# Layer 1's transformed signs at a row pitch of 32 words, and the high weight parts in float16 on the words' upper halves

## The chip, the cores and the metric

The kernel runs on one core of a Trainium2 chip. The metric is the device time of one execution in microseconds (us); three runs of the kernel before took 992.37, 992.5 and 993.49, median 992.5.

## The reference

Four layers are applied one after another to x of 16 images with 256 channels of 28 x 28. Layer 0 is a 3x3 convolution of signs with signs of weights and a batch norm. Layer 1, which the change concerns, is this (bn with stored moments is a scale s and a shift c per channel):

```
residual = prelu(x, a_alpha1)
z = hardsign(x + a_move)                      # sign(x): -1, 0 or 1
bw = clip(a_w, -1.0, 1.0)
y = conv_general_dilated(z, bw, 3x3, padding 1)
y = prelu(bn(y, a_bn1), a_alpha2)
y = se_gate(...) * y * residual
y = bn(y, a_bn2) + residual
z2 = hardsign(y + f_move)
u = einsum('bchw,oc->bohw', z2, clip(f_w))    # a 1x1 convolution
u = bn(se_gate(...) * prelu(bn(u, f_bn1), f_alpha2), f_bn2)
return u + y
```

Layer 2 is two more 3x3 convolutions of signs with batch norms, layer 3 attention over the 784 pixels of each image. In layer 1 the signs are whole numbers, but the weights are not[...].

## The kernel before

All work is on one core, and in stages: layer 0 to about 120 us, layer 1 from 123.6 to about 490 us, the two convolutions of layer 2 to about 700 us, and attention. The order of the instructions on TensorE (PE), VectorE (DVE) and ScalarE (ACT) is written out by hand in each stage (`manual_schedule`); on the queue of SyncE (SP) loads are issued, on that of GpSimd (POOL) stores of finished images.

**The convolution of layer 1.** It is computed by a transform over pairs of rows. From the padded signs of an image (`pads`, bfloat16), `transform` (DVE; the operation itself stands in the helper `tt`, so the profile shows L134) makes four sets u = 0 to 3 of 14 rows, sums or differences of two rows, with values between -2 and 2, and puts them into `vs`. This tile holds, in float32r (32-bit words[...]), for two images in turn, four sets and two groups of 128 channels, 14 rows of 30 words (28 columns and one more at each side). Set u is convolved along the row only, with three taps c = 0, 1, 2; the row of tap c begins c words later. The transformed weights are split into a high part `w1[0]`, rounded to float32r, and a low part `w1[1]`, the rest, both in float32r; this is done in layer 0, four pieces at a time: the sums of taps on DVE, `high` on ACT (L512), `low` on DVE (L516), in the list of side steps that `sign_layer` interleaves with the blocks of layer 0. `conv` (L699) sums over two channel groups k, the two parts and three taps: 12 matmuls of 128x128 weights with 128x392 rows into one half of an accumulator:

```
for k in range(2):
    for w in w1:
        for c in range(3):
            T.matmul(ps..., lhsT=w[:, k, c, u, mo*P:(mo+1)*P],
                     rhs=vs[:, b % 2, u, k, :, c:c + S], ...)
```

So three high matmuls alternate with three low ones. An image has two halves mo of output channels with four sets u each: 8 convolutions, 96 matmuls; 16 images make 1536.

**An iteration of layer 1** (`iteration(b)`) carries three images at different steps. PE's order: convolutions u = 1, 2 for mo = 0 (the first pair), u = 0, two small products (L618, hidden layer of the gates), u = 3, two small products (L778, gates), u = 1, 2, 0, 3 for mo = 1, and the 1x1 convolution of the image before (`conv1x1`, L809, 16 matmuls, also in float32r, with 392 words in a row). A pair shares one accumulator tile of two banks ("cv"). There are three such tiles and an iteration uses six, so a pair waits until the tile of three uses earlier is read out. The first pair of the next iteration reuses that of u = 0, 3 with mo = 1.

ACT takes t = s1 * (first of pair) + c1 (`sum_pair_a`, L720); DVE then makes t + s1 * (second) and t - s1 * (second) (`sum_pair_b`, L730, into `uvs`), and when u = 0, 3 are done adds these in (`rows_out`, L739), which frees the tile. Between these DVE has, for the neighbouring images, `enter` (L663), `prelu` (L751), `residual_b` (L691, which needs rn of ACT's L657), four transforms, `branch1_b` (L794) and `branch2` (L831). In iterations 1 to 6 it also packs signs of layer 2's second weights (`signs3`, L267), whose ACT results go through a stage tile of the tag "sgb".

When the operation counts its own doubts to be too large, a second, careful pass of the whole forward function follows; its `careful` branches are not run here.

Of the kernel before, what the change touches and what calls it, by code (L numbers as in the profile page):

```python
# [27 lines left out]
F32 = mybir.dt.float32  # L28
FR = mybir.dt.float32r
F16 = mybir.dt.float16  # L30
BF16 = mybir.dt.bfloat16
I16 = mybir.dt.int16
I32 = mybir.dt.int32
AF = mybir.ActivationFunctionType
ALU = mybir.AluOpType
# [4 lines left out]
P = 128  # L40
B = 16
S = 28
N = S * S
HN = N // 2
HR = S // 2
# [38 lines left out]
def forward(ctx: ExitStack, tc: tile.TileContext, d: dict, out: bass.AP, careful: bool):  # L84
# [4 lines left out]
    V, A, T = nc.vector, nc.scalar, nc.tensor  # L89
# [11 lines left out]
    def pv(name):  # L101
        return vec[:, VECS.index(name), :]
# [27 lines left out]
    def vtile(name):  # L130
        return const.tile([P, 2], F32, name=name)

    def tt(o, a, b, op):
        V.tensor_tensor(o, a, b, op)  # L134
        return o
# [284 lines left out]
    with tc.tile_pool(name="ps_conv", bufs=3, space=PSUM) as psc, \  # L420
# [13 lines left out]
        with tc.tile_pool(name="ph1", bufs=1) as ph:  # L434
# [51 lines left out]

            w1 = [ph.tile([P, 2, 3, 4, 256], FR, name=f"w1_{i}") for i in range(2)]
            fw = [ph.tile([P, 2, 256], FR, name=f"fw_{i}") for i in range(2)]  # L490

            def w1_step(k, c):
                sts, parts = [], []

                def load():
                    sts.append(xpool.tile([P, 3, 256], F32, tag="x2", name="st", bufs=3))
                    nc.sync.dma_start(out=sts[0], in_=d["w1"][k, :, c::3, :])

                def sums_of_taps():
                    st = sts[0]  # L500
                    V.tensor_scalar(st, st, -1.0, 1.0, ALU.max, ALU.min)
                    t = ph.tile([P, 3, 256], F32, tag="rn", name="asm", bufs=2)
                    a, s, m = (t[:, i, :] for i in range(3))
                    tt(a, st[:, 0, :], st[:, 2, :], ALU.add)
                    tt(s, a, st[:, 1, :], ALU.add)
                    tt(m, a, st[:, 1, :], ALU.subtract)
                    for u, (w, f) in enumerate(((st[:, 0, :], 1.0), (s, 0.5), (m, 0.5), (st[:, 2, :], -1.0))):
                        parts.append((w, f, *(x[:, k, c, u, :] for x in w1)))

                def high():  # L510
                    for w, f, hi, lo in parts:
                        A.activation(hi, w, AF.Copy, scale=f)  # L512

                def low():
                    for w, f, hi, lo in parts:
                        V.scalar_tensor_tensor(lo, w, f, hi.bitcast(F32), ALU.mult, ALU.subtract)  # L516

                return Step(load, sums_of_taps), high, low

# [12 lines left out]
            s1, s2, s3, s4 = (s_bn[:, i, :] for i in range(4))  # L532
            c1, c2, c3, c4 = (c_bn[:, i, :] for i in range(4))
            cc, zb2 = vtile("cc"), vtile("zb2")
            ra1, ra2, rf2, ns1 = (vtile(q) for q in ("ra1", "ra2", "rf2", "ns1"))
            mix_x, mix_y, mix_c = (const.tile([P, 2, 2], F32, name=n) for n in ("mix_x", "mix_y", "mix_c"))

            w_1, w_2, b_1 = (ph.tile(sh, F32, name=n) for sh, n in (([P, 2, P], "se1"), ([P, 256], "se2"), ([64, 1], "seb")))
# [4 lines left out]
            def constants():  # L543
                for p in pads:
                    nc.gpsimd.memset(p, 0.0)
                nc.gpsimd.tensor_copy(
                    doubts[:, 4 * NB:4 * NB + 6], vec[:, VECS.index("a1"):VECS.index("a3") + 1, :].rearrange("p i k -> p (i k)")
                )
                for i, n in enumerate(("a_alpha2", "f_alpha2")):
                    nc.gpsimd.tensor_copy(doubts[:, 4 * NB + 6 + 2 * i:4 * NB + 8 + 2 * i], pv(n))  # L550
                v = const.tile([P, 4, 2], F32, name="v_bn")
                for i, bn in enumerate(bns):
                    V.tensor_scalar(v[:, 2 * i:2 * i + 2], bn[:, 3::4], EPS, None, ALU.add)
                r = rsqrt("bn", v)
                for i, bn in enumerate(bns):
                    two = slice(2 * i, 2 * i + 2)
                    tt(s_bn[:, two], bn[:, 0::4], r[:, two], ALU.mult)
                    tt(c_bn[:, two], bn[:, 2::4], s_bn[:, two], ALU.mult)
                    tt(c_bn[:, two], bn[:, 1::4], c_bn[:, two], ALU.subtract)
                tt(cc, c2, c4, ALU.add)  # L560

                for o, q in ((ra1, "a_alpha1"), (ra2, "a_alpha2"), (rf2, "f_alpha2")):
                    V.tensor_scalar(o, pv(q), -1.0, 1.0, ALU.mult, ALU.add)
                V.tensor_scalar(ns1, s1, -1.0, None, ALU.mult)
                tt(zb2, c2, pv("f_move"), ALU.add)
                for g, (q, scale) in enumerate((("a", pv("a_scale")), ("f", pv("f_scale")))):
                    V.tensor_scalar(mix_x[:, g], scale, 1.0 / N, None, ALU.mult)
                    V.tensor_scalar(mix_y[:, g], scale, -1.0 / N, 1.0 / N, ALU.mult, ALU.add)
                    rows = slice(32 * g, 32 * g + 32)
                    nc.sync.dma_start(out=w_1[:, :, rows], in_=d[f"se1_{q}"])  # L570
                    nc.sync.dma_start(out=w_2[rows], in_=d[f"se2_{q}"])
                    nc.sync.dma_start(out=b_1[rows], in_=d[f"seb_{q}"])
                    nc.sync.dma_start(out=w_2[64 + 32 * g:65 + 32 * g], in_=d[f"seb2_{q}"])
                tt(mix_c[:, 1], pv("f_scale"), c2, ALU.mult)
# [48 lines left out]
                    rows = slice(32 * g, 32 * g + 32)  # L623
                    tt(b_1[rows], h, b_1[rows], ALU.add)

            vs = ph.tile([P, 2, 4, 2, HR, S + 2], FR, tag="vs", name="vs")

            def room_sums():
                return ph.tile([P, PIECE], F32, tag="sts", name="sts", bufs=2)

            if not careful:
                w2b = packed_weights(wpool, tag="wb")
                signs3 = sign_weights(ph, w2b, d["w2b"], ("sts", 2), sg=("sgb", 1))
            sums12 = weight_sums(room_sums, d["w2a_rows"], sf1, 6) + weight_sums(room_sums, d["w2b_rows"], sf2, 12)

            sums = {}
# [36 lines left out]
            def transform(b, u, k=slice(0, 2)):  # L673

                rows = pads[b % 2].rearrange("p k (i two) c -> p k two i c", two=2)
                e, o = rows[:, :, 0], rows[:, :, 1]
                e0, e1, o0, o1 = e[:, :, 0:HR], e[:, :, 1:HR + 1], o[:, :, 0:HR], o[:, :, 1:HR + 1]
                x, y, op = (
                    (e0, e1, ALU.subtract), (o0, e1, ALU.add), (e1, o0, ALU.subtract), (o0, o1, ALU.subtract)
                )[u]  # L680
                tt(vs[:, b % 2, u, k], x[:, k], y[:, k], op)

            rx = {}

# [8 lines left out]
            def conv(b, mo, u, ps):  # L693

                n = 0
                for k in range(2):
                    for w in w1:
                        for c in range(3):
                            T.matmul(  # L699
                                ps.rearrange("p (a b) -> p a b", b=S),  # L700
                                lhsT=w[:, k, c, u, mo * P:(mo + 1) * P],
                                rhs=vs[:, b % 2, u, k, :, c:c + S],
                                start=(n == 0),
                                stop=(n == 11),
                            )
                            n += 1
# [4 lines left out]
            pairs = {}  # L711
# [6 lines left out]
            def sum_pair_a(b, mo):  # L718
                t = temp("t1")[:, :HN]
                A.activation(  # L720
                    t, pairs[b, mo, True][:, 0, :HN], AF.Identity, bias=c1[:, mo:mo + 1], scale=s1[:, mo:mo + 1]
                )
                pairs[b, mo] = t

            def sum_pair_b(b, mo):

                ps, t = pairs.pop((b, mo, True)), pairs.pop((b, mo))
                uv = uvs[:, mo]
                for i, s in enumerate((s1, ns1)):
                    V.scalar_tensor_tensor(uv[:, i], ps[:, 1, :HN], s[:, mo:mo + 1], t, ALU.mult, ALU.add)  # L730
                pairs[b, mo] = uv

            def rows_out(b, mo):
                ps, uv = pairs.pop((b, mo, False)), pairs.pop((b, mo))
                y = full("yu", f"y{b}_{mo}", 6)
                ys[b, mo] = y
                two = y.rearrange("p (a two b) -> p two a b", two=2, b=S)
                for i in range(2):
                    V.scalar_tensor_tensor(  # L739
                        two[:, i], ps[:, i, :HN].rearrange("p (a b) -> p a b", b=S), s1[:, mo:mo + 1],  # L740
                        uv[:, i].rearrange("p (a b) -> p a b", b=S), ALU.mult, ALU.add,
                    )

# [203 lines left out]
            with tc.manual_schedule(engines={ET.PE, ET.DVE, ET.Activation}):  # L947
# [21 lines left out]
                b = B - 1  # L969
# [74 lines left out]
        with tc.tile_pool(name="ph2", bufs=1) as ph:  # L1044
            if careful:
                w2b = packed_weights(ph, tag="wb")
# [687 lines left out]
```

## Time and profile before

| | us |
|---|---|
| runs | 992.37, 992.5, 993.49 (median 992.5) |
| profiled execution, its own time | 991.88 |
| its span in the trace | 989.8 |
| PE busy, all of the kernel | 959.3 |
| DVE busy | 799.7 |
| ACT busy | 676.6 |
| layer 1's convolution (L699), PE busy, 1536 matmuls | 301.4 |
| 1x1 convolution (L809), PE busy, 256 matmuls | 49.1 |
| iteration 0 of layer 1 (123.62 to 142.32) | 18.7 |
| iterations 1 to 14, each | 21.9 to 22.0 |

How to read it: the profiler records one execution. "Busy" of PE is the union of its matmuls; these overlap, so the mean duration of one is longer than the distance between the starts of two, and it is that distance which adds up in a stream. PEld are the loads of weights, which lie beside the matmuls. A group's line gives the source line, engine, operation, output <- inputs, shapes, count, then busy us and mean ns of one, and behind the second bar the idle time of the engine before these instructions with what ended it. A timeline line gives start, duration, engine, line and operation, and in brackets the idle time before and what released it. Lines L134 and L148 are helpers, named with the tiles they work on. The granted clock of TensorE is full in layer 1 (1.00 in each stretch).

### The profile page before, as it was taken

How to read it: one execution, taken by the hardware profiler on the slowest of the kernel's cores; microseconds unless marked ns; L12 is line 12 of the kernel's file. 1: busy time of each engine (PE TensorE's matmuls, PEld its weight loads, DVE VectorE, ACT ScalarE, POOL GpSimd, SP SyncE). 2: the span in 40 equal slices, each digit the busy share in tenths (PEclk: the TensorE clock that was granted, in tenths of full speed). 3: DMA queues.
4: the chain of work that ended last, by engine and by line, in shares of the span. 5: the costliest groups of instructions: out<-in, count | busy, mean ns of one | idle time of the engine just before them, and what ended most of it. 6: DMA issues, size and time to landing. Idle time of an engine off the chain costs nothing.

```text
span 989.8 us, 14752 instructions
## 1 busy us (share of the span) xinstructions
PE 959.3 (97%) x5609; PEld 662.7 (67%) x5615; DVE 799.7 (81%) x1416; ACT 676.6 (68%) x1135; POOL 140.9 (14%) x149
## 2 busy tenths in 40 slices
PE   7999899999999999999999999999999999999995
PEld 3555499999999999999555555555444444444442
DVE  4766998999999899996779997999847777777765
ACT  6787437677776666664688877888676666666652
POOL 3000100000000000000000000000054434444430
PEclk9999999999999999999999999999999999999998
DMA  9877512334343322101291000000034252525212
GB/s 348 323 256 282 180 46 85 114 114 140 132 142 114 106 98 82 66 33 53 101 404 62 1 1 1 1 2 1 1 66 98 66 131 66 131 66 130 66 66 102
DMA packets 26949, 105.82 MB, mean 107 GB/s; under 512 B 3491, under 2 KB 7269, under 8 KB 26869
## 3 DMA queue, kind: packets, MB, share of 16 engines
q1 hardware_dynamic: 20948, 73.44, 20.8%
q0 software_dynamic: 5632, 30.54, 11.3%
q8 instruction: 46, 0.75, 0.3%
q10 hardware_dynamic: 288, 0.80, 0.2%
q14 instruction: 35, 0.28, 0.1%
HBM read 72.67 MB, written 32.11 MB: 106 GB/s over the span
## 4 chain that ended last, share of the span: by engine, by line
PE 45%; DVE 4%; ACT 1%; issue 1%; DVEq 0%; ACTq 0%
PE cv L340 19%; PE sc L1309 8%; PE av L1330 8%; PE mi L1286 4%; PE sm L1372 2%; PE mi L1390 2%; PE sm L1330 1%; DVE p L1096 1%; DVE r L1356 1%; DVE ab L354 0%; DVE l2c_fin L1098 0%; DVE l2b_fin L1098 0%; DVE p L1273 0%; PE sc L1390 0%; DVE p L1272 0%
## 5 line engine op out<-in xcount | busy, mean ns | idle before, releaser
L340 PE MATMUL cv<-fpads,wpk 128*128 128x392 f16 (+1 forms) x1746 | 295.7, 331 | 10.1 <-ACT fpads L451 5.1
L699 PE MATMUL cv<-vs,w 128*128 128x392 f32 x1536 | 301.4, 354 | 3.0 <-DVE vs L134 3.0
L699 PEld LDWEIGHTS cv<-vs,w 128*128 128x128 f32 x1536 | 287.3, 190 | 4.8 <-issue 3.4
L340 PEld LDWEIGHTS <-wpk 128*128 128x128 f16 x1746 | 168.9, 97 | 137.3 <-issue 9.8
L1313 ACT ACTIVATE es<-sc 128x784 f32<-128x784 f32 x112 | 87.3, 822 | 41.7 <-PE sc L1309 41.7
L1309 PE MATMUL sc<-q,keyswa 64*128 64x392 f32 x448 | 89.9, 513 | 0.9 <-ACT es L1313 0.9
L1096 DVE SCALAR_TENSOR_TENSOR p<-ab,vec 128x392 f32<-128x392 f32 x128 | 79.1, 618 | 2.3
L1330 PE MATMUL av<-es,v 128*64 128x392 f32 x448 | 80.7, 499 | 0.0
L1309 PEld LDWEIGHTS sc<-q,keyswa 64*128 64x128 f32 x448 | 38.9, 186 | 43.9 <-issue 17.1
L1323 POOL TENSOR_TENSOR sum<-sum,es 128x784 f32<-128x784 f32 x32 | 67.2, 2100 | 3.1 <-ACT es L1313 0.7
L134 DVE TENSOR_TENSOR vs<-pad 128x840 fp32r<-128x840 bf16 (+1 forms) x66 | 64.4, 1000 | 0.1
L1330 PEld LDWEIGHTS av<-es,v 128*64 128x64 f32 x448 | 29.4, 136 | 47.3 <-issue 47.0
L837 POOL DMA_DIRECT2D x2d<-x x16 | 8.6, 536 | 358.3 <-DVE x L831 295.0
L1297 DVE COPY keyswa<-mi 64x392 f32<-64x392 f32 x31 | 16.3, 565 | 52.5 <-ACT q L1293 52.5
L720 ACT ACTIVATE t<-cv,c_bn,s_bn 128x392 f32<-128x392 f32 x32 | 21.7, 678 | 49.9 <-PE cv L699 49.9
L351 ACT ACTIVATE t<-cv,rounding 128x392 f32<-128x392 f32 (+2 forms) x82 | 51.6, 630 | 4.9 <-PE cv L340 1.9
L1101 ACT ACTIVATE t<-ab 128x392 f32<-128x392 f32 x64 | 33.5, 524 | 27.8 <-DVE ab L354 27.8
L809 PE MATMUL cv<-z,fw 128*128 128x392 f32 x256 | 49.1, 343 | 1.0 <-ACT z L801 0.9
L354 DVE SCALAR_TENSOR_TENSOR ab<-ab,cv 128x392 f32<-128x392 f32 x64 | 35.4, 554 | 17.6 <-ACT ab L352 17.6
L809 PEld LDWEIGHTS cv<-z,fw 128*128 128x128 f32 x256 | 46.0, 188 | 2.2 <-ACT z L801 2.2
L1286 PE MATMUL mi<-p,wqk 128*128 128x392 f32 x124 | 45.3, 506 | 0.3 <-DVE p L1273 0.3
L1321 POOL TENSOR_TENSOR sum<-es 128x784 f32<-128x784 f32 x16 | 30.0, 1877 | 91.0 <-ACT es L1313 91.0
(284 smaller groups left out, 1462.7 us busy)
## 6 DMA issues: line engine op xcount, KB each, us to landing
xs<-in_x_dram SPq DMA_DIRECT2D x30, 784.0 KB, 6.8
x2d<-x POOLq DMA_DIRECT2D x16, 784.0 KB, 3.8
out_dram<-p SPq DMA_DIRECT2D x15, 784.0 KB, 3.7
p<-x2d POOLq DMA_DIRECT2D x14, 784.0 KB, 6.8
p<-x2d SPq DMA_DIRECT2D x13, 784.0 KB, 15.9
n0d<-n POOLq DMA_DIRECT2D x16, 392.0 KB, 4.8
n<-n0d SPq DMA_DIRECT2D x16, 392.0 KB, 3.1
st<-in_w_dram SPq DMA_DIRECT2D x12, 384.0 KB, 6.2
```

What stands on the lines that cost most here:

```text
L134: V.tensor_tensor(o, a, b, op)
L340: T.matmul(pss[j][:, n // size if careful else h, :rows * S].rearrange("p (a b) -> p a b", b=S), lhsT=w[:, n, t, :], rhs=pads[:, blocks[j] ...
L351: A.activation(by_halves(t, blocks[j]), ps, AF.Identity, bias=rounding, scale=1.0 / PACK)
L354: V.scalar_tensor_tensor(a, b, -PACK, ps, ALU.mult, ALU.add)
L699: T.matmul(ps.rearrange("p (a b) -> p a b", b=S), lhsT=w[:, k, c, u, mo * P:(mo + 1) * P], rhs=vs[:, b % 2, u, k, :, c:c + S], start=(n == 0),
L809: T.matmul(ps[:, h, :HN], lhsT=w[:, k, mo * P:(mo + 1) * P], rhs=z2[b][:, k, h * HN:(h + 1) * HN], start=(k + i == 0), stop=(k + i == 2),)
L1096: V.scalar_tensor_tensor(p, y, alpha[:, mo:mo + 1], y, ALU.mult, ALU.max)
L1286: T.matmul(ps[:, h, :HN], lhsT=wqk[:, k, :], rhs=x[b][:, k, h * HN:(h + 1) * HN], start=(k == 0), stop=(k == 1))
L1309: T.matmul(ps[:, h, :HN], lhsT=chunk[rows], rhs=qs[b][rows], start=True, stop=True)
L1313: A.activation(e, ps[:, :, :HN], AF.Exp, scale=0.125)
L1323: (V if late else nc.gpsimd).tensor_tensor(sums[b, late], sums[b, late], e, ALU.add)
L1330: T.matmul(ps[64 * h:64 * h + 64, :HN], lhsT=w, rhs=e[:, h, :], start=start, stop=stop)
```

## The change

The rows of `vs` stand at a pitch of 32 words in place of 30 (`WIDE = S + 4`; columns 0 to 29 are written, 30 and 31 are never read). The high part `w1[0]` becomes float16; so that small values keep their digits, high and low part are both made 2^15 times as large (`UP`), and the scales that read the accumulators are divided by that (`us1`, one DVE operation more, and `ns1`). The high matmuls don't read the float32r words but `vs16`, a bfloat16 view of the same tile that takes the upper half of each word; values between -2 and 2 in steps of one are the same in it. The low matmuls read the words as before. In the compiled program the float16 weights have load instructions of their own in PE's list, while a float32r matmul brings its load with it; otherwise the order of the work on PE, ACT, DVE, POOL and SP is the same. The stage tile of `signs3` takes the tag "sg" that layer 0's `signs2` used before it.

```diff
+            HI = FR if careful else F16
+            UP = 1.0 if careful else 2.0**15
-            w1 = [ph.tile([P, 2, 3, 4, 256], FR, name=f"w1_{i}") for i in range(2)]
+            w1 = [ph.tile([P, 2, 3, 4, 256], dt, name=f"w1_{i}") for i, dt in enumerate((HI, FR))]
...
                 def high():
                     for w, f, hi, lo in parts:
-                        A.activation(hi, w, AF.Copy, scale=f)
+                        A.activation(hi, w, AF.Copy, scale=f * UP)
 
                 def low():
                     for w, f, hi, lo in parts:
-                        V.scalar_tensor_tensor(lo, w, f, hi.bitcast(F32), ALU.mult, ALU.subtract)
+                        V.scalar_tensor_tensor(
+                            lo, w, f * UP, hi.bitcast(F32) if careful else hi, ALU.mult, ALU.subtract
+                        )
...
-                V.tensor_scalar(ns1, s1, -1.0, None, ALU.mult)
+                V.tensor_scalar(us1, s1, 1.0 / UP, None, ALU.mult)
+                V.tensor_scalar(ns1, s1, -1.0 / UP, None, ALU.mult)
...
-            vs = ph.tile([P, 2, 4, 2, HR, S + 2], FR, tag="vs", name="vs")
+            WIDE = S + 4
+            vs = ph.tile([P, 2, 4, 2, HR, WIDE], FR, tag="vs", name="vs")
+            vs16 = vs.rearrange("p b u k i c -> p (b u k i c)").bitcast(BF16).rearrange(
+                "p (b u k i c two) -> p b u k i c two", b=2, u=4, k=2, i=HR, two=2
+            )[..., 1]
...
-                signs3 = sign_weights(ph, w2b, d["w2b"], ("sts", 2), sg=("sgb", 1))
+                signs3 = sign_weights(ph, w2b, d["w2b"], ("sts", 2), sg=("sg", 1))
...
-                tt(vs[:, b % 2, u, k], x[:, k], y[:, k], op)
+                tt(vs[:, b % 2, u, k, :, 0:S + 2], x[:, k], y[:, k], op)
...
-                    for w in w1:
+                    for w, v in zip(w1, (vs if careful else vs16, vs)):
                         for c in range(3):
                             T.matmul(
                                 ps.rearrange("p (a b) -> p a b", b=S),
                                 lhsT=w[:, k, c, u, mo * P:(mo + 1) * P],
-                                rhs=vs[:, b % 2, u, k, :, c:c + S],
+                                rhs=v[:, b % 2, u, k, :, c:c + S],
```

In `sum_pair_a`, `sum_pair_b` and `rows_out`, `us1` takes the place of `s1`.

More of the change, by code (lines that the diff above doesn't have):

```diff
@@ L534, in forward @@
             cc, zb2 = vtile("cc"), vtile("zb2")
-            ra1, ra2, rf2, ns1 = (vtile(q) for q in ("ra1", "ra2", "rf2", "ns1"))
+            ra1, ra2, rf2, us1, ns1 = (vtile(q) for q in ("ra1", "ra2", "rf2", "us1", "ns1"))
             mix_x, mix_y, mix_c = (const.tile([P, 2, 2], F32, name=n) for n in ("mix_x", "mix_y", "mix_c"))
@@ L720, in sum_pair_a @@
                 A.activation(
-                    t, pairs[b, mo, True][:, 0, :HN], AF.Identity, bias=c1[:, mo:mo + 1], scale=s1[:, mo:mo + 1]
+                    t, pairs[b, mo, True][:, 0, :HN], AF.Identity, bias=c1[:, mo:mo + 1], scale=us1[:, mo:mo + 1]
                 )
@@ L728, in sum_pair_b @@
                 uv = uvs[:, mo]
-                for i, s in enumerate((s1, ns1)):
+                for i, s in enumerate((us1, ns1)):
                     V.scalar_tensor_tensor(uv[:, i], ps[:, 1, :HN], s[:, mo:mo + 1], t, ALU.mult, ALU.add)
@@ L739, in rows_out @@
                     V.scalar_tensor_tensor(
-                        two[:, i], ps[:, i, :HN].rearrange("p (a b) -> p a b", b=S), s1[:, mo:mo + 1],
+                        two[:, i], ps[:, i, :HN].rearrange("p (a b) -> p a b", b=S), us1[:, mo:mo + 1],
                         uv[:, i].rearrange("p (a b) -> p a b", b=S), ALU.mult, ALU.add,
```

## The prediction

> **What bounds the kernel now.** I read the page first, for the shares of the engines and the costliest groups:
>
> ```profile
> PE 959.3 (97%) x5609; PEld 662.7 (67%) x5615; DVE 799.7 (81%) x1416; ACT 676.6 (68%) x1135; POOL 140.9 (14%) x149
> ...
> L340 PE MATMUL cv<-fpads,wpk 128*128 128x392 f16 (+1 forms) x1746 | 295.7, 331 | 10.1 <-ACT fpads L451 5.1
> L699 PE MATMUL cv<-vs,w 128*128 128x392 f32 x1536 | 301.4, 354 | 3.0 <-DVE vs L134 3.0
> L699 PEld LDWEIGHTS cv<-vs,w 128*128 128x128 f32 x1536 | 287.3, 190 | 4.8 <-issue 3.4
> L340 PEld LDWEIGHTS <-wpk 128*128 128x128 f16 x1746 | 168.9, 97 | 137.3 <-issue 9.8
> ...
> L809 PE MATMUL cv<-z,fw 128*128 128x392 f32 x256 | 49.1, 343 | 1.0 <-ACT z L801 0.9
> ```
>
> The convolution of layer 1 (L699) keeps TensorE busy for 301.4 us and makes it wait for only 3.0. Its mean of 354 ns is the latency of one matmul; what a matmul costs in a stream is the distance between starts. Read from the trace's single starts, that distance has these typical values: L699 189.5 ns; L809, the same float32r but with 392 words in a row, 179.5; L340, float16 with 28 of 30 elements a row, 165, and 177 for the tap whose rows begin at an odd half word. By tap and address the L699 groups lie between 185.4 and 194.4.
>
> Next I read the busy time of the engines by stage, one stretch an iteration of layer 1 (iterations 4, 7, 9):
>
> ```profile
> core 0: us, PE busy (x) PEld busy (x) DVE busy (x) ACT busy (x) POOL busy (x), PEclk, DMA share, GB/s
> ...
> 208.15:230.12 21.97, 21.97 (x122) 21.88 (x122) 20.68 (x40) 15.56 (x25) 0.53 (x1) 1.00 0.39 128
> ...
> 274.01:295.95 21.94, 21.94 (x122) 21.86 (x121) 21.06 (x44) 15.47 (x24) 0.53 (x1) 1.00 0.37 125
> ...
> 317.92:339.85 21.93, 21.93 (x122) 21.86 (x121) 20.17 (x41) 14.91 (x23) 0.53 (x1) 1.00 0.32 110
> ```
>
> PE is busy for the whole period of 21.95 us, so it is the bound. But DVE is at 20.2 to 21.1 of the 21.95: PE can gain little more than 1 us an iteration before DVE takes over. Last, the timeline of iteration 9 shows where the two meet:
>
> ```profile
> 317.92 6.98 PE L699 MATMUL cv<-vs,w 128*128 128x392 f32 x36
> ...
> 322.66 0.68 ACT L720 ACTIVATE t<-cv,c_bn,s_bn 128x392 f32<-128x392 f32 x1 [2.70 <-PE cv L699]
> ...
> 323.37 0.63 DVE L730 SCALAR_TENSOR_TENSOR uvs<-cv,s_bn,t 128x392 f32<-128x392 f32 x1 [1.18 <-ACT t L720]
> ...
> 324.73 0.50 PE L618 MATMUL hid<-g,se 128*128 128x2 f32 x4
> ...
> 326.80 1.03 DVE L691 SCALAR_TENSOR_TENSOR xs<-rn,ra,xs 128x784 f32<-128x784 f32 x1 [0.38 <-ACT rn L657]
> ...
> 337.82 1.15 DVE L739 SCALAR_TENSOR_TENSOR y<-cv,s_bn,uvs 128x392 f32<-128x392 f32 x2
> ...
> 339.85 0.55 PE L699 MATMUL cv<-vs,w 128*128 128x392 f32 x2
> ```
>
> DVE waits 1.18 us for the first pair of convolutions (24 matmuls, then t on ACT) and 0.38 for rn. PE's next iteration begins at 339.85, 0.9 us after DVE freed its accumulator at 338.97 (the third of three buffers).
>
> **Is L699 bound by its weight loads or by its moving rows?** The load's 190 ns look like the bound, but are not. Where 2-column matmuls follow one another (L618), weights of the same size and type come at starts 111 ns apart. And the distance belongs to the matmul that is streaming: L699 followed by L618 184 to 190, L809 followed by L699 176 to 186 and mostly 177, whatever is loaded next. So the rows streamed set the 189.5. A change of number type costs nothing visible: the bfloat16 matmul of 512 columns ahead of L618 takes 216 ns as among its own, and L809 ahead of a bfloat16 one 183.
>
> [...] no run here shows a strided 16-bit moving operand.
>
> **The change part by part.**
>
> *High parts in float16 (768 of the 1536 matmuls).* They stream bfloat16 from the upper half of each word, 4 bytes apart. Bounds: 165 (L340), to 329, the distance of L1286[...]. I take 168, L340's mean over all its taps[...]. Loading in float16 costs 97 instead of 190, worth nothing by itself as loads are hidden; the cover is a matmul of over 165 ns. Saving: 189.5 − 168 = 21.5 ns each.
>
> *Pitch of 32 words (the 768 low matmuls).* Rows then begin alike. Bounds: 179.5 (L809, no row breaks) and 194.4 (the slowest of L699's groups). I take 186, a third of the way from 189.5 to 179.5. Saving: 3.5 each.
>
> *PE's period.* Before: 96 × 189.5 + 16 × 180 + 0.9 for the small matmuls = 18.19 + 2.88 + 0.9 = 21.97 (21.95 seen). After: 48 × 168 + 48 × 186 = 16.99; with 2.88 + 0.9, 20.77.
>
> *What is late next.* (a) DVE: 21.95 less the 1.18 wait = 20.77. (b) The loop through the accumulators: from DVE's L730 at 323.37 to the end of L739 at 338.97 are 15.60; then PE's 24 matmuls at 177 are 4.25, 0.19 to t, 0.71 from t's start to L730, some 0.06 for the release: 20.81 (before: 21.11, not binding). So a usual iteration takes about 20.81 and saves 1.14. In iterations 3 to 7 DVE also signs weights or adds sums (20.6 to 21.1 busy, its wait at L730 only 0.70 in iteration 4): I take 21.0, saving 0.95.
>
> *Sum.* Iteration 0, PE alone: 96 × 12.5 ns = 1.2. Iterations 1, 2 and 8 to 14: 9 × 1.14 = 10.3. Iterations 3 to 7: 4.75. Iteration 15, in which PE also waits 0.9 for others: 0.9. In all 17.1.
>
> *The small edits.* One 128x2 operation more on DVE at the end of layer 0: its twin (L564) takes 160 ns and starts 70 to 110 apart from its neighbours; I take 0.1, fully on the path. Of the transforms (DVE, 1025 ns), only the output gets row breaks; L739 with row breaks (617) costs as much as L730 without (616 to 623), so nothing; at 30 ns each it would be 0.12 an iteration, 1.9 in all. L512 and L516 (some 0.41 each) write and read float16 in layer 0, where PE is the bound: nothing, at most 0.1. The scale of 2^15 is folded into existing scales. The sharing of the stage for signs moves no instruction: on ACT, POOL and SP the order of the work and the DMAs are the same, and the layer 0 user of that stage is long done.
>
> The profiled execution took 991.88 (span 989.8, 2.1 around it), 0.6 below the median of 992.5. 991.9 − 17.0 = 974.9; on the median's scale 975.5.
>
> **Rivals.**
> 1. *The halves are read at the speed of whole words* (chance 0.23). If float32r is slow because of 4 bytes a column, the strided halves[...] gain no more than the pitch gives: 96 × 3.5 ns × 16 = 5.4 us, 987; between 980 (both near 180) and 993 (pitch worth nothing). For it: L809 and L699 differ from 165 only in the word's size. Against it: the load of 128 float32 weights beside the stream, which float16 halves, may be what disturbs it.
> 2. [...] (0.18), the one on the other side. The 177 against 165 of the odd tap is 12 ns over 14 rows[...]. Then every strided half costs[...] the 329 of L1286. PE bound throughout: 768 × 139.5 ns = +107.1, less 2.7 for the pitch: 1097. It decides from a high matmul of 193 ns on (193 + 186 = 2 × 189.5).[...]
> 3. DVE as a harder bound than reckoned is a lower gain inside the first case: with 21.25 in all usual iterations 0.7 × 16 = 11, 981.
>
> **Numbers.** The forecast (high about 165 to 178) has 0.59, its own range 968 to 984: at 165 and 179.5 PE needs 20.3, loop and DVE hold it at 20.5 to 20.7, saving 22 to 24; at 177 and 189.5 the period is 21.37, saving 9. The range over two cases: 968 to 994, leaving out rival 2 and little else. A measurement of this kernel tells about 0.2% (2 us) from no change. Faster: 0.59 + 0.13 of rival 1 = 0.72; within: 0.07 of rival 1; slower: 0.18 + 0.03 of rival 1 (a pitch that disturbs more, or DVE's transforms) = 0.21.
>
> **What would show it.** Starts of high matmuls 165 to 170 apart, of low ones near 186, the period near 20.8, DVE's wait at L730 nearly gone and PE waiting at the first pair for DVE's L739. High starts at 180 to 190 show rival 1; at 329, rival 2. Wrong would also be a low group above 190 or transforms above 1025 ns.

## The result, and the profile after

The changed kernel takes 996.68 us (median of five runs, 994.77 to 997.81), the kernel before 992.37 beside it: 1.0043 times as long, with a 95% interval of 1.0028 to 1.0057. The prediction had 975.5 and a range of 968 to 994. The change was meant to relieve TensorE in layer 1, and made it slower there.

The page of the changed kernel (L699 is now L708, L809 is L818):

```profile
PE 963.9 (97%) x5615; PEld 574.1 (58%) x5615; DVE 801.0 (81%) x1417; ACT 676.6 (68%) x1135; POOL 141.1 (14%) x149
...
L708 PE MATMUL cv<-vs,w 128*128 128x392 bf16 (+1 forms) x1536 | 306.7, 386 | 2.6 <-DVE vs L134 2.6
...
L708 PEld LDWEIGHTS cv<-vs,w 128*128 128x128 f32 x768 | 143.9, 190 | 27.7
...
L708 PEld LDWEIGHTS <-w 128*128 128x128 f16 x768 | 57.8, 102 | 68.9 <-issue 44.8
...
L818 PE MATMUL cv<-z,fw 128*128 128x392 f32 x256 | 49.1, 343 | 1.0 <-ACT z L810 0.9
```

The loads did what was asked of them: half are float16, and PEld's busy time falls from 662.7 to 574.1 us. The matmuls did not follow: 306.7 us in place of 301.4. New is the second load line's idle time, 44.8 us of "issue", in which the weight loader waited for nothing that the profile shows.

Busy time of the engines in iteration 9 of the changed kernel:

```profile
core 0: us, PE busy (x) PEld busy (x) DVE busy (x) ACT busy (x) POOL busy (x), PEclk, DMA share, GB/s
320.65:342.94 22.29, 22.29 (x122) 16.40 (x121) 20.20 (x39) 14.91 (x23) 0.53 (x1) 1.00 0.32 108
```

PE is still busy throughout, and the period is 22.29 us in place of 21.95; DVE does the same 20.2 us of work in it. The timeline of the same iteration:

```profile
320.65 7.18 PE L708 MATMUL cv<-vs,w 128*128 128x392 bf16 x36
...
322.21 0.57 PEld L708 LDWEIGHTS cv<-vs,w 128*128 128x128 f32 x3
...
322.98 0.29 PEld L708 LDWEIGHTS <-w 128*128 128x128 f16 x3 [0.21 <-issue]
...
326.24 0.63 DVE L739 SCALAR_TENSOR_TENSOR uvs<-cv,us,t 128x392 f32<-128x392 f32 x1 [1.44 <-ACT t L729]
...
340.76 1.15 DVE L748 SCALAR_TENSOR_TENSOR y<-cv,us,uvs 128x392 f32<-128x392 f32 x2
...
342.94 0.55 PE L708 MATMUL cv<-vs,w 128*128 128x392 bf16 x2
```

36 matmuls take 7.18 us in place of 6.98, DVE waits 1.44 us for the first pair in place of 1.18, and each return from float32r to float16 shows the loader idle for some 0.2 us. From the first to the last start of the 3x3 convolution the two traces have 348.9 and 354.4 us. The span grew by only 2.9, mainly since the profiled execution of the kernel before took 22.9 us after its last scores in attention and this one 20.6; nothing of the change works there, and the medians differ by 4.3. The granted clock can't be the cause: it is 1.00 from 150 to 440 us in every trace here, of this kernel, of the one before and of the experiments.

Distances between the starts of single matmuls carry the rest. A float32r matmul that follows a float16 one is recorded some 29 ns after it, so only the sum of two distances can be read ("h2+l0"). Medians in ns, read from the single starts of each trace; h are the high matmuls of taps 0, 1, 2, l the low ones, "six" one channel group; "period" is that of a usual iteration in us:

| kernel | h0 | h1 | h2+l0 | l1 | l2 | six | period |
|---|---|---|---|---|---|---|---|
| before | 189 | 190 | 378 | 190 | 189 | 1140 | 21.95 |
| changed | 192 | 197 | 380 | 195 | 206 | 1169 | 22.29 |
| e1, pitch 32 alone | 187 | 196 | 391 | 196 | 204 | 1173 | 22.52 |
| e2, halves, pitch 30 | 195 | 190 | 373 | 190 | 192 | 1140 | 21.83 |
| e3, packed high, pitch 32 | 180 | 177 | 350 | 193 | 205 | 1106 | 21.26 |

### The profile page after: what moved, and what is told of

Its sections match the earlier page's. It is cut to its first block, busy times and chain, and to the rows that moved or that the text cites. A ratio compares the mean times of both kernels' runs of the same rounds, so it can differ in the third digit from the quotient of the medians.

```text
span 992.7 us, 14740 instructions
## 1 busy us (share of the span) xinstructions
PE 963.9 (97%) x5615; PEld 574.1 (58%) x5615; DVE 801.0 (81%) x1417; ACT 676.6 (68%) x1135; POOL 141.1 (14%) x149
## 3 DMA queue, kind: packets, MB, share of 16 engines
q1 hardware_dynamic: 20948, 73.44, 20.8%
## 4 chain that ended last, share of the span: by engine, by line
PE 45%; DVE 3%; ACT 1%; issue 1%; DVEq 0%; ACTq 0%
PE cv L340 19%; PE sc L1318 8%; PE av L1339 8%; PE mi L1295 4%; PE sm L1381 2%; PE mi L1399 2%; PE sm L1339 1%; DVE p L1105 1%; DVE ab L354 0%; ACT es L1322 0%; DVE l2b_fin L1107 0%; DVE l2c_fin L1107 0%; DVE r L1365 0%; DVE p L1282 0%; DVE p L1281 0%
## 5 line engine op out<-in xcount | busy, mean ns | idle before, releaser
L708 PE MATMUL cv<-vs,w 128*128 128x392 bf16 (+1 forms) x1536 | 306.7, 386 | 2.6 <-DVE vs L134 2.6
L340 PE MATMUL cv<-fpads,wpk 128*128 128x392 f16 (+1 forms) x1746 | 295.7, 331 | 9.9 <-ACT fpads L451 5.0
L340 PEld LDWEIGHTS <-wpk 128*128 128x128 f16 x1746 | 169.0, 97 | 137.0 <-issue 9.9
L708 PEld LDWEIGHTS cv<-vs,w 128*128 128x128 f32 x768 | 143.9, 190 | 27.7
L708 PEld LDWEIGHTS <-w 128*128 128x128 f16 x768 | 57.8, 102 | 68.9 <-issue 44.8
L729 ACT ACTIVATE t<-cv,c_bn,us 128x392 f32<-128x392 f32 x32 | 21.7, 678 | 52.9 <-PE cv L708 52.9
L818 PE MATMUL cv<-z,fw 128*128 128x392 f32 x256 | 49.1, 343 | 1.0 <-ACT z L810 0.9
L818 PEld LDWEIGHTS cv<-z,fw 128*128 128x128 f32 x256 | 46.0, 188 | 2.4 <-ACT z L810 2.2
```

Of the source, the lines that this page charges most:

```text
L340: T.matmul(pss[j][:, n // size if careful else h, :rows * S].rearrange("p (a b) -> p a b", b=S), lhsT=w[:, n, t, :], rhs=pads[:, blocks[j] ...
L708: T.matmul(ps.rearrange("p (a b) -> p a b", b=S), lhsT=w[:, k, c, u, mo * P:(mo + 1) * P], rhs=v[:, b % 2, u, k, :, c:c + S], start=(n == ...
L818: T.matmul(ps[:, h, :HN], lhsT=w[:, k, mo * P:(mo + 1) * P], rhs=z2[b][:, k, h * HN:(h + 1) * HN], start=(k + i == 0), stop=(k + i == 2),)
```

## The experiments

**Two parts apart: e1 and e2.** e1 is the kernel before with the pitch alone, e2 the changed kernel at the old pitch.

```diff
# e1, on the kernel before
-vs = ph.tile([P, 2, 4, 2, HR, S + 2], FR, tag="vs", name="vs")
+vs = ph.tile([P, 2, 4, 2, HR, S + 4], FR, tag="vs", name="vs")
...
-tt(vs[:, b % 2, u, k], x[:, k], y[:, k], op)
+tt(vs[:, b % 2, u, k, :, 0:S + 2], x[:, k], y[:, k], op)
...
-sg=("sgb", 1)
+sg=("sg", 1)
# e2, on the changed kernel
-WIDE = S + 4
+WIDE = S + 2
```

Expected of e1:

> The kernel before with the pitch of 32 words alone (both weight parts float32r). Before: float32r matmuls 189.5 ns apart, an iteration of layer 1 takes 21.95 us, 992.4 us in all. If the pitch helps as the prediction took it: 186 ns apart, 21.6 us an iteration, 987. If the pitch itself is what slowed the change: about 195 ns apart, as two of the low matmuls of the changed kernel are, 22.45 us an iteration, 1000. If it does nothing: 21.95 and 992.

Expected of e2:

> The changed kernel with rows at a pitch of 30 words again, the high part still float16 on the upper halves. Changed kernel: 22.29 us an iteration, 996.7 us. If the speed of whole words is what the halves are read at, and the pitch is worth nothing: again about 22.3 us and 996 to 997. If the pitch of 32 cost time: 21.9 us or less, 991. If the pitch of 32 helped: over 22.4 us, 999 or more.

e1: 1000.39 us, 1.0076 times before (1.0059 to 1.0093), an iteration 22.52. e2: 990.08, 0.9978 times (0.9969 to 0.9986), an iteration 21.83. The matmul groups of e1 and of e2:

```profile
L699 PE MATMUL cv<-vs,w 128*128 128x392 f32 x1536 | 311.4, 364 | 3.9 <-DVE vs L134 3.9
```

```profile
L708 PE MATMUL cv<-vs,w 128*128 128x392 bf16 (+1 forms) x1536 | 299.4, 378 | 3.1 <-DVE vs L134 3.1
```

The pitch is what costs (301.4 to 311.4 us of PE). The shared stage tile ("sg"), which e1 takes over from the change, is not: e2 shares it too and is not slower. The float16 halves give a little back: 0.12 us an iteration at the old pitch, 0.2 at the new one. The two parts pull against each other.

**What a half word costs: e3, e4, e6.** e3 reads neighbouring 16-bit elements for the high part, e4 the lower halves, e6 makes both parts float16 halves at a pitch of 30.

```diff
# e3, on the changed kernel: the view vs16
-    "p (b u k i c two) -> p b u k i c two", b=2, u=4, k=2, i=HR, two=2
-)[..., 1]
+    "p (b u k i c) -> p b u k i c", b=2, u=4, k=2, i=HR
+)
# e4, on the changed kernel
-)[..., 1]
+)[..., 0]
# e6, on e2
-for i, dt in enumerate((HI, FR))]
+for i, dt in enumerate((HI, HI))]
...
-zip(w1, (vs if careful else vs16, vs))
+zip(w1, (vs, vs) if careful else (vs16, vs16))
```

Expected of e3:

> The changed kernel, but the high matmuls read 28 neighbouring 16-bit elements a row (the first 14 to 15 words of each row, both halves) in place of the upper halves of 28 words. This changes the values that the high part multiplies: it is for the time only. Theory A (a strided half costs as much as a whole word): high matmuls 165 to 177 ns apart, 168 on average; with 190, 195 and 205 for the low ones 1094 ns for six, 21.3 us an iteration, 981. Theory B (the alternation of float16 and float32r, with the loads that float16 weights have of their own, is what costs): no change, 22.3 us and 997.

Expected of e4:

> The changed kernel, with the lower halves of the words in place of the upper ones, so that each row begins at a whole word for tap 0 and no element at an odd half word. The lower halves are zeros, so the high part is left out of the result: for the time only. If the odd half word costs time ([...]12 ns a matmul, on three of six): 21.7 us an iteration, 988. If only the four bytes a column count: 22.3 us, 997, as the changed kernel.

Expected of e6:

> Both weight parts in float16, both read from the upper halves at a pitch of 30 words; no float32r matmul and no float32 weight load is left in the 3x3 convolution. If four bytes a column set the time, whatever is loaded beside it: 184 to 190 ns a matmul, 21.4 to 22 us an iteration, 985 to 992. If the load of float32 weights beside the stream was what slowed it: 165 to 168, 20.8 us with DVE as the bound, 975.

The matmul group of e3:

```profile
L708 PE MATMUL cv<-vs,w 128*128 128x392 bf16 (+1 forms) x1536 | 291.5, 372 | 2.7 <-DVE vs L134 2.7
```

e3: 980.36, 0.9878 times before (0.9861 to 0.9894), an iteration 21.26. Theory A had 21.3 and 981, theory B 22.3 and 997: A holds. Theory B, the alternation of types, is left with little, which e5 measures below. e4: 997.65 in one run, an iteration 22.29, with the distances of the changed kernel to within 1 ns: which half is read, and that it starts at an odd place, doesn't matter. e6: 981.81 in one run, an iteration 21.46; the taps take 184, 189 and 184 ns, the mean 186. The groups of e6:

```profile
L708 PE MATMUL cv<-vs,w 128*128 128x392 bf16 x1536 | 293.4, 348 | 2.7 <-DVE vs L134 2.7
...
L708 PEld LDWEIGHTS <-w 128*128 128x128 f16 x1536 | 147.9, 99 | 134.2 <-DVE vs L134 3.2 <-issue 2.5
```

Every load there is float16 and the loader stands idle 134 us, yet a matmul takes 186 and not 168. So the float32 load beside the stream isn't what makes four bytes a column slow; a strided half is read at nearly the speed of a whole word (186 against 189.5). The 3.5 ns between 186 and 189.5 lie at taps 0 and 2 (184 against some 189); tap 1 takes 189 where it took 190 to 192. Whether they come from the number type or from the lighter load isn't separated.

**The change of number type: e5.** On e2, a convolution's six high matmuls come first, then its six low ones.

```diff
-for k in range(2):
-    for w, v in zip(w1, (vs if careful else vs16, vs)):
+for w, v in zip(w1, (vs if careful else vs16, vs)):
+    for k in range(2):
         for c in range(3):
```

> Upper halves at a pitch of 30 words, but the six high matmuls of a convolution come first and the six low ones after them, so that the number type changes once and back in twelve matmuls instead of twice. With three and three: 21.83 us an iteration, 990.1; the first high matmul of a group is some 6 to 15 ns slower than the second. If each change from float32r to float16 costs about 15 ns (the float16 load starts only when the float32r matmul is nearly through): 8 changes fewer an iteration, 21.71 us, 988. If the change costs nothing: 21.83 and 990.

988.2 us, 0.9964 times before (0.9948 to 0.998), an iteration 21.70: 0.13 less than e2 for 8 changes fewer, some 15 ns each. (The medians of the two kernels alone are too close to tell them apart; the iterations, steady to 0.03 us, do.) The single starts of the changed kernel show what is different there. Elsewhere a float16 load starts some 2 to 12 ns after the start of the matmul before its own, a whole matmul ahead. Where that matmul is a float32r one, the load starts 202 ns after its start, when it is nearly through, and only 4 ns before the load's own matmul. That this late load causes the 15 ns fits, but isn't shown; why a load of some 100 ns then costs no more stays open.

**Why the pitch costs: e8, e9, e11, e12.** e8 moves the columns by two words at a pitch of 32; e9 is the changed kernel at 34 words, e12 the kernel before at 31; e11 has no padding at all.

```diff
# e8, on e1
-tt(vs[:, b % 2, u, k, :, 0:S + 2], x[:, k], y[:, k], op)
+tt(vs[:, b % 2, u, k, :, 2:S + 4], x[:, k], y[:, k], op)
...
-rhs=vs[:, b % 2, u, k, :, c:c + S],
+rhs=vs[:, b % 2, u, k, :, c + 2:c + 2 + S],
# e9, on the changed kernel
+WIDE = S + 2 if careful else S + 6
# e12, on e1
+vs = ph.tile([P, 2, 4, 2, HR, S + 2 if careful else 31], FR, tag="vs", name="vs")
# e11, on the kernel before (the transform writes columns 0 to 27)
+vs = ph.tile([P, 2, 4, 2, HN + 4], FR, tag="vs", name="vs")
...
+rhs=vs[:, b % 2, u, k, c:c + HN].rearrange("p (a b) -> p a b", b=S),
```

Expected of e8:

> The pitch of 32 words alone, both parts float32r, with the columns moved by two words in the row: tap c begins at word c + 2 instead of c. Without the move the three taps take 187, 196 and 204 ns. If the place of a row's start[...] sets the cost: word 2 again 204, word 3 about 200 to 210, word 4 again 187; an iteration between 22.5 and 22.8 us. If the cost grows with the distance from the start of the 128 bytes: 204, 213, 221, an iteration of 24 us, 1030.

Expected of e9:

> The changed kernel with a pitch of 34 words (136 bytes, two words past a multiple of four, as 30 words are). If what costs at 32 is that every row begins at the same place[...]: as at 30, low matmuls 188 to 192 for every tap, 21.8 us an iteration, 990. If what costs is rows that lie further apart: as at 32 or worse, 22.3 us or more, 997.

Expected of e11:

> The kernel before (float32r throughout), but each row of the transformed signs has 28 words and no padding, so that a matmul reads 392 words in a row from word c on; at the ends of rows the taps take the neighbouring row's value, so the borders are wrong: for the time only. [...] 180 to 182 ns for all three taps, 21.15 us an iteration, 980. If the breaks do nothing: 189.5, 21.95, 992.

Expected of e12:

> The kernel before with a pitch of 31 words, both parts float32r; [...]three words are passed over between two rows (two at a pitch of 30, four at 32). If the words passed over set the cost, it lies between: about 192 to 193 ns a matmul, 22.2 us an iteration, 997. If what costs is that all rows begin at the same place[...]: as at 30 or better, 189.5 and 21.95 us, 992.

e8: 1001.76 in one run, 22.53 us an iteration; words 2, 3 and 4 take 200, 202 and 184 ns. Word 2 is near the 204 and word 4 near word 0's 187 of e1: the place in a group of four words counts at this pitch, not the distance from the row's start. e9: 1002.56 in one run, 22.44 us; the low taps 1 and 2 take 195 to 198. So rows that begin alike are not what costs: 34 words, two past a multiple of four as 30 are, are no better than 32. e12: 995.64 in one run, 22.2 us, 190 to 195 ns. e11: 978.36 in one run, 21.05 us, all taps near 180. Its groups:

```profile
L703 PE MATMUL cv<-vs,w 128*128 128x392 f32 x1536 | 288.1, 345 | 3.9 <-DVE vs L134 3.9
L703 PEld LDWEIGHTS cv<-vs,w 128*128 128x128 f32 x1536 | 275.6, 189 | 4.8 <-issue 4.3 <-DVE y L743 0.3
L134 DVE TENSOR_TENSOR vs<-pad 128x784 fp32r<-128x784 bf16 (+1 forms) x66 | 60.7, 944 | 0.1
```

Over the runs in float32r, a matmul's mean rises with the words passed over between two rows: none 180, two 189.5, three 192, four 195.5 ns.

**Is DVE next? e10.** e6 with the packed view of e3 at a pitch of 30: packed reads for all matmuls, transforms unchanged.

```diff
-)[..., 1]
+)
```

(with "p (b u k i c) -> p b u k i c" as the view)

> Both parts in float16 as in the run with all halves, pitch of 30 words, transforms still written in float32r; but the matmuls read 28 neighbouring 16-bit elements a row. The signs that they read are not those of the convolution: for the time only. Matmuls at 165, 177, 165 ns; PE would need 20.0 us. If the prediction's second step holds (DVE and the accumulator loop are next, at 20.7 to 20.8 us): 20.8 us an iteration, 974, with PE waiting. If not: 20.0 us, 963.

972.39 in one run; usual iterations 20.5 to 20.7, two of 21.0. The groups from 140 to 440 us, which hold its iterations 1 to 14, then busy times of iterations 4 and 11, and the start of iteration 11:

```profile
L708 PE MATMUL cv<-vs,w 128*128 128x392 bf16 x1414 | 251.4, 334 | 3.5 <-DVE y L748 3.5
...
L134 DVE TENSOR_TENSOR vs<-pad 128x840 fp32r<-128x840 bf16 x58 | 58.3, 1027 | 0.0
```

```profile
core 0: us, PE busy (x) PEld busy (x) DVE busy (x) ACT busy (x) POOL busy (x), PEclk, DMA share, GB/s
205.55:226.23 20.68, 20.34 (x120) 12.92 (x120) 20.48 (x40) 15.51 (x25) 0.54 (x1) 1.00 0.42 136
350.14:370.66 20.52, 20.35 (x120) 12.94 (x120) 20.13 (x39) 14.79 (x24) 0.53 (x1) 1.00 0.35 118
```

```profile
350.14 0.85 PE L708 MATMUL cv<-vs,w 128*128 128x392 bf16 x4 [0.18 <-DVE y L748]
```

The taps take 168, 178 and 173 ns, and PE is busy for 20.3 us an iteration. The rest of the period it waits for DVE's L748, at the place that the prediction had named for it (the release of the accumulator). DVE itself has 0.2 to 0.4 us to spare, so of the prediction's two bounds the loop through the accumulators is the one that shows; with 173 ns in it, it comes to 20.7.

**A version that beats both: e7.** The signs themselves are written in bfloat16 and read packed, both weight parts are float16.

```diff
# on the changed kernel
-vs = ph.tile([P, 2, 4, 2, HR, WIDE], FR, tag="vs", name="vs")
-vs16 = ...
+vs = ph.tile([P, 2, 4, 2, HR, S + 2], FR if careful else BF16, tag="vs", name="vs")
...
-for i, dt in enumerate((HI, FR))]
+for i, dt in enumerate((HI, HI))]
...
-zip(w1, (vs if careful else vs16, vs))
+zip(w1, (vs, vs))
```

> What the runs so far point to: the transformed signs themselves in bfloat16 (60 bytes a row), both weight parts in float16 times 2^15, no float32r in the 3x3 convolution. If the bytes read a column set the time: matmuls 165, 177, 165 ns for the three taps, PE needs 96 x 169 + 16 x 180 + 0.9 us = 20.0 us an iteration. If DVE's transforms stay at 1025 ns, DVE and the accumulator loop hold it at 20.8: 974. If they get faster with bfloat16 on both sides[...]: 20.0 to 20.2, 963 to 966. If the words' width is not the cause: about 189 ns and no gain, 990.

959.49 us, 0.9663 times before (0.965 to 0.9677); an iteration 19.91; taps 166, 177, 166 ns. The groups from 140 to 440 us, which hold its iterations 1 to 14:

```profile
L704 PE MATMUL cv<-vs,w 128*128 128x392 bf16 x1443 | 252.7, 333 | 0.0
...
L134 DVE TENSOR_TENSOR vs<-pad 128x840 bf16<-128x840 bf16 x58 | 33.0, 590 | 0.0
```

The transforms fall from 1025 to 590 ns and so lift DVE out of the way; the 3x3 convolution waits for nothing in iterations 1 to 14 (0.0 us idle). The matmuls are 3 ns faster than in e10 too, whose rows lie twice as far apart.

## Why the prediction was wrong

**What bounds the kernel: right.** The loads aren't the bound: in e6 they fall to 99 ns and a matmul still takes 186, and in e11 loads of 189 ns stand beside matmuls 180 apart. The matmuls' moving rows are, and PE sets the period. e11 shows also that L809's 179.5 against L699's 189.5 lies in the row breaks.

**The high matmuls at 168: wrong, the largest term.** In six matmuls the prediction had 3 x 168 + 3 x 186 = 1062 ns; the trace has 1169. Taking 195.5 for each low matmul from e1 and 15 for the change of type from e5, the three high ones have 1169 − 586.5 − 15 = 567.5, or 189 each (an estimate). The same sum at a pitch of 30, with 189.5 for a low one, is 1140 − 568.5 − 15 and gives 185; e6 measured 186. With packed halves the parts add up as well: 504 + 586.5 + 15 = 1105.5, and e3 has 1106. That is rival 1: halves read at about the speed of whole words. Its counter-argument, that the float32 load disturbs the stream, fell with e6. That a strided half streams like L340's packed elements was the author's estimate; no run before the change showed a strided 16-bit operand. With rows at the same pitch of 30 words, 16-bit elements four bytes apart take 184 to 189 ns (e6) and neighbouring ones 168 to 178 (e10). Rival 2, 329 ns for a high matmul, is excluded.

**The pitch at 186: wrong in sign.** The bound below was sound (e11 has 180 without breaks), but a wider pitch leads away from it: 195.5. The prediction read "rows begin alike" as an advantage with no line of the profile for it. The upper bound of 194.4, the slowest group, was close; for single taps it was passed (204), and a low group above 190 was what the prediction itself had named as a sign of being wrong. Of the missing 107 ns this term is 3 x 9.5 = 29, the high matmuls 567.5 − 504 = 63, the change of type 15.

**"A change of number type costs nothing visible": wrong.** The evidence was one step from float32r to bfloat16 (183 ns) beside a range of 176 to 186 for that predecessor, too coarse for 15 ns, and it didn't ask when the explicit load is issued.

**What is late next: right in kind, though it never came to it.** e10 is held by the accumulators at 20.5 to 20.7 us, where 20.8 had been reckoned. **The small edits: nothing to see.** The transforms take 1028 ns, before 1026.

So two losses, the pitch and the change of type, met a gain that was some 4 to 6 ns a high matmul in place of 21.5. With e1 and e2 they add up: +7.5 us for the pitch (1000.39 against 992.92), −2.8 for the halves at the old pitch, +4.7; measured +4.3.

**Open:** why a pass over more words costs. The word at which the rows begin doesn't explain it alone. At a pitch of 32, words 0 and 4 take 184 to 187 ns, and words 1, 2 and 3 take 196, 200 to 204 and 202. But at a pitch of 30 words 0, 1 and 2 take 189 to 190 (before), and with a pitch of 34, also two words past a multiple of four, the low taps 1 and 2 take 195 to 198. Nor do the runs separate whether a strided half is slow for the distance of its elements or for the bytes that a row spans.

## What to carry to other kernels

Ask what a matmul's moving operand spans in bytes, not how many bits of each element it uses: to gain from a 16-bit type, store it packed (166 to 177 ns in e7, where halves of words took 184 to 189 in e6). A bound that is read off two shapes (with and without row breaks) says where to go only when the change moves towards the better one; widening a pitch moves away from it (180 ns without breaks, 189.5 at 30 words, 195.5 at 32). And where matmuls of two types alternate, look in the loader's row for "issue" at each return (some 0.2 us here).

## What the runs showed of the hardware that was not expected

- A moving operand of 392 columns, four bytes apart, takes 180 ns without row breaks, and 189.5, 192 and 195.5 with two, three and four words passed over at each of 14 rows; within a pitch of 32 it takes 184 to 204 by the word at which the rows begin.
- Taking the half of each word saves some 4 ns of 189.5 at a pitch of 30 words, nearly all of it at taps 0 and 2 (184 against some 189). Packing saves some 20 (e7), and 17 with the rows 120 bytes apart (e10).
- A return from a float32r matmul to a float16 one costs some 15 ns; the float16 load then starts about 0.2 us after the matmul before it did, where it starts 2 to 12 ns after it elsewhere.
- A DVE addition or subtraction of 840 bfloat16 elements takes 1025 ns when it writes float32r and 590 when it writes bfloat16.
